# Layer 1's normalised inputs, from the third sequence on, transposed by VectorE in 32 x 32 squares that change places through DRAM instead of by TensorE

## The chip, the cores and the metric

The kernel runs on one core of a Trainium2 chip. The metric is the device time of one execution in microseconds (us). Engines are named as in the profile: PE is TensorE (PEld its weight loads), DVE is VectorE, ACT is ScalarE, POOL is GpSimd, SP is SyncE, which here only issues DMAs. SBUF is the memory on the core with 128 partitions, PSUM the accumulators of TensorE (8 banks of 128 x 512 f32), DRAM the memory off the core.

## What is computed

Two layers over x of shape (8, 512, 256): 8 sequences of 512 tokens with 256 channels, all f32. Layer 1 has causal attention with 16 heads of 64 and rotated queries and keys, and beside it a projection of the same normalised input in int8. Layer 2 has an attention of another kind and a gated network; the change does not touch what it computes. Cut to what matters:

```python
xn = layernorm(x)
q, k, v = xn @ Wq + bq, xn @ Wk + bk, xn @ Wv + bv          # 16 heads of 64
attended = softmax(causal(rope(q) @ rope(k).T / 8)) @ v
s = max(abs(xn).max() / 127, 1e-5)                          # over all sequences
quantised = (clip(round(xn / s), -128, 127) @ w8.T) * s * weight_scale + bias
x = x + attended @ Wo + bo + quantised                      # layer 1
yn = layernorm(x)
x = x + mask * softmax(left @ right.T / 16 + gate_bias) @ yn + gated(yn)   # layer 2
```

Every projection contracts over channels. A matmul of TensorE contracts over partitions, so the normalised input, which comes with tokens on partitions, is needed with channels on partitions: xnT, two halves k of 128 channels, each with 512 tokens along the partition. The projection of queries and keys streams xnT (the moving operand, with the weights stationary); the projection of values loads xnT as the stationary operand; the int8 projection uses a rounded and clipped copy of it as the stationary operand.

## The kernel before

The order of the instructions of each engine is the order of the program text; no scheduler moves anything within layer 1 and layer 2's body. An engine runs its instructions in that order and waits on semaphores; so does SP with its DMAs. All loads and stores below go through SP's one queue.

Layer 1 is a loop over 16 steps "at" (line 813), two for each sequence: b = at // 2 is the sequence, g = at % 2 the half of its heads. A step computes scores for its 8 heads in five runs, softens them (exponentials), turns the probabilities in squares of 32 on DVE (L551), and weighs the values of the step before. Between these lie the projections for later steps:

- project(at + 1, 0) makes queries for the next step, project_v(at + 1) its values, and project(at + 2, 1), near the end of the step, the keys of the step after next. All of these go through project_qk (L400 the matmuls, L405 their eviction by ACT, L407 four DMAs each that swap halves of heads) and project_v (L443 matmuls, L449 eviction, L450 a store to DRAM; load_v, L460, reads it back with 32 partitions to a DMA in the next step).
- prepare(b) normalises a sequence (L171) and takes the greatest magnitude (L301). From the fourth sequence on it runs in the step before its transposes; for the third it runs in the same step (at == 2), just ahead of them.
- transpose_x(b + 1) runs in the first step of a sequence (g == 0), after project_v(at + 1) and ahead of scores(at, 3): eight 128 x 128 transposes on PE (L318) into two PSUM banks, two copies by ACT into xnT (L321), and one DMA that keeps xnT in DRAM (keep_input, L310) for the int8 projection later. Then SP loads x of the next sequence (L80) into the only buffer that there is for x.

The first reader of the new xnT is project(at + 2, 1) of the same step, after scores(at, 3), scores(at, 4) and finish(at - 1) (L362, the output projection). xnT has two buffers (pool "big"), one for each of two sequences in flight.

The first two sequences are transposed ahead of the loop (lines 756 and 795). The kept inputs are read back much later: for sequences 0 and 1 in steps last - 3 and last - 2 (line 834), for sequence 2 in the last step (line 931), for the others in the loop of layer 2 (fetch_late). Each is rounded by POOL (L190), clipped by DVE (L196, L197) into bf16 and multiplied (L205). The buffer tag "xnl" holds such a late input; one of soften's tiles uses it once, in step 0.

Of the kernel before, what the change touches and what calls it, by code (L numbers as in the profile page):

```python
# [8 lines left out]
F32 = mybir.dt.float32  # L9
BF16 = mybir.dt.bfloat16  # L10
I8 = mybir.dt.int8
AF = mybir.ActivationFunctionType
ALU = mybir.AluOpType
# [3 lines left out]
P = 128  # L17
B, S, D = 8, 512, 256
H, L = 16, 64
NT = S // P  # L20
NK = D // P
# [8 lines left out]
Q = 32  # L30
# [10 lines left out]
ROUND = 12582912.0  # L41
# [3 lines left out]
def two_layers(  # L45
    ctx: ExitStack, tc, x, turns, Wq, Wk, Wv, Wo, w8, rows, sides, second, gates, out,
):
    nc = tc.nc
# [3 lines left out]
    big = ctx.enter_context(tc.tile_pool(name="big", bufs=2))  # L52
# [4 lines left out]
    far = ctx.enter_context(tc.tile_pool(name="far", bufs=1, space=bass.MemoryType.DRAM))  # L57
    ps = ctx.enter_context(tc.tile_pool(name="ps", bufs=8, space=PSUM))

    def bank(name):  # L60
        return ps.tile([P, S], F32, tag="b", name=name)

    def whole(name, columns=S):
        t = big.tile([P, NK * (S + 1)], F32, tag="big", name=name)
        return t[:, : NK * columns].rearrange("p (k n) -> p k n", k=NK)

    def tokens(b):
        return x[b].rearrange("(t p) c -> p t c", p=P)
# [2 lines left out]
        return xpool.tile([P, NT, D], F32, tag="x1", name=name, bufs=3)  # L71

    x1_far = [far.tile([P, NT * D], F32, name=f"x1f_{b}") for b in range(B - 1)]
    xn_far = [far.tile([P, NK * S], F32, name=f"xnf_{b}") for b in range(B)]

    def load_x(b, parts=1):
        t = xpool.tile([P, NT, D], F32, tag="x", name=f"x_{b}")
        for h in range(parts):
            rows = slice(h * NT // parts, (h + 1) * NT // parts)
            nc.sync.dma_start(t[:, rows, :], tokens(b)[:, rows, :])  # L80
        return t
# [8 lines left out]
    x_next = [load_x(0, 2)]  # L90
# [37 lines left out]
    w8b = const.tile([P, NK, D], BF16, name="w8b")  # L128
# [52 lines left out]
        nc.sync.dma_start(dst.rearrange("p t n -> p (t n)"), x1_far[b])  # L181

    def fetch_input(b, r):
        nc.sync.dma_start(r.rearrange("p a n -> p (a n)"), xn_far[b])
        return r

    def round_input(r):

        r = r.rearrange("p a n -> p (a n)")
        nc.gpsimd.tensor_scalar(r, r, xs[:, 1:2], ROUND, ALU.mult, ALU.add)  # L190

    def clip(r, xq):

        r = r.rearrange("p a n -> p (a n)")
        xq_ = xq.rearrange("p k n -> p (k n)")
        nc.vector.tensor_scalar(xq_, r, -ROUND, -128.0, ALU.add, ALU.max)  # L196
        nc.vector.tensor_scalar(xq_, xq_, 127.0, 127.0, ALU.min, ALU.min)  # L197

    def add_quantised(b, half, xq, u):
        rows = slice(2 * half, 2 * half + 2)  # L200
        acc = bank(f"acc_{b}_{half}").rearrange("p (j n) -> p j n", j=2)
        for j in range(2):
            tok = bass.ts(2 * half + j, P)
            for k in range(NK):
                nc.tensor.matmul(  # L205
                    acc[:, j, :], xq[:, k, tok], w8b[:, k, :], start=(k == 0), stop=(k == NK - 1)
                )
        u = u.rearrange("p (j n) -> p j n", j=2)
        for j in range(2):
            nc.vector.scalar_tensor_tensor(  # L210
                u[:, j, :], acc[:, j, :], xs[:, 0:1], rw[:, 0, :], ALU.mult, ALU.mult
            )
        nc.gpsimd.tensor_tensor(x1s[b][:, rows, :], x1s[b][:, rows, :], u, ALU.add)
# [41 lines left out]
    with ExitStack() as c0:  # L255
        c0.enter_context(tc.manual_schedule())

        def pool(name, bufs, **kw):
            return c0.enter_context(tc.tile_pool(name=name, bufs=bufs, **kw))

        work = pool("work", 1)
# [8 lines left out]
        wo = work.tile([P, NP, D], F32, name="wo")  # L270
# [15 lines left out]
        xnT = {}  # L286
        amax = work.tile([P, B], F32, name="amax")

        normed, seen = {}, {}
# [15 lines left out]
        def prepare(b):  # L305
            norm_input(b)
            greatest_of(b)

        def keep_input(b):
            nc.sync.dma_start(xn_far[b], xnT[b].rearrange("p k n -> p (k n)"))  # L310

        def transpose_x(b):
            xn = normed.pop(b)
            xnT[b] = whole(f"xnT_{b}")
            for k in range(NK):
                pb = bank(f"pxt_{b}_{k}")
                for t in range(NT):
                    nc.tensor.transpose(  # L318
                        pb[:, bass.ts(t, P)], xn[:, t, bass.ts(k, P)], ident
                    )  # L320
                nc.scalar.copy(xnT[b][:, k, :], pb)  # L321
            if b > 0:
                keep_input(b)

# [62 lines left out]
        def project_qk(at, which):  # L387


            b, g = divmod(at, NG)  # L390
            w = wqkv[which]

            l, y = (
                prob.tile([P, 2, S], F32, tag="p", name=f"{tag}_{at}_{which}") if at == 1 else
                work.tile([P, 2, S], F32, tag=tag, name=f"{tag}_{at}_{which}", bufs=2) for tag in "ly"
            )
            for t in range(2):
                pb = bank(f"pq_{at}_{which}_{t}")
                for k in range(NK):
                    nc.tensor.matmul(  # L400
                        pb, w[:, g, k, bass.ts(t, P)], xnT[b][:, k, :],
                        start=(k == 0), stop=(k == NK - 1),
                    )
                bias = BIAS + which * NP + 2 * g + t
                nc.scalar.activation(l[:, t, :], pb, AF.Identity, bias=cs[:, bias : bias + 1])  # L405
            for n in range(4):
                nc.sync.dma_start(y[bass.ts(n ^ 1, Q)], l[bass.ts(n, Q)])  # L407
            evicted[at, which] = l, y
# [25 lines left out]
        def project_v(at, halves=(0, 1)):  # L434
            b, g = divmod(at, NH)
            if 0 in halves:
                stores[at] = away.tile([4, P, NT * P], F32, tag="v", name=f"va_{at}")
            for half in halves:
                v = work.tile([P, 4, 2, P], F32, tag="v", name=f"v_{at}_{half}", bufs=2)
                for j in range(2):  # L440
                    pb = bank(f"pv_{at}_{half}_{j}")
                    for k in range(NK):
                        nc.tensor.matmul(  # L443
                            pb.rearrange("p (g n) -> p g n", g=2),
                            xnT[b][:, k, bass.ts(2 * half + j, P)],
                            wqkv[2][:, 2 * g : 2 * g + 2, k, :],
                            start=(k == 0), stop=(k == NK - 1),
                        )
                    nc.scalar.copy(v[:, :, j, :], pb.rearrange("p (r n) -> p r n", r=4))  # L449
                nc.sync.dma_start(  # L450
                    stores[at][:, :, half * 2 * P : half * 2 * P + 2 * P].rearrange("r p n -> p r n"),
                    v.rearrange("p r t n -> p r (t n)"),
                )
# [103 lines left out]
        half = S // Q // 2  # L557
# [28 lines left out]
        cuts = {}  # L586
# [7 lines left out]
        def by_tokens(t):  # L594
            return t.rearrange("p (t n) -> p t n", t=NT)

        late = {}

        def fetch_late(b):
            if b < B - 1:  # L600
                tag, k = {2: ("vr", 0), 3: ("vr", 1), 4: ("t1", 0), 5: ("t1", 1), 6: ("t2", 0)}[b]
                fetch_output(b, by_tokens(cuts[tag][k]))
            if b > 2:
                late[b] = fetch_input(b, cuts["wo"][b % 2].rearrange("p (k n) -> p k n", k=NK))

        def round_late(b):
            round_input(late[b])

        def clip_late(b):
            xq = work.tile([P, NK, S], BF16, tag="xq", name=f"xq_{b}")  # L610
            clip(late.pop(b), xq)
            return xq

# [199 lines left out]
        for at in range(1, last):  # L813
            b, g = divmod(at, NH)
# [16 lines left out]
            if at in (last - 3, last - 2):  # L831
                s_ = at - last + 3
                fetch_output(s_, output_tile(f"x1e_{s_}"))
                xnl = fetch_input(s_, work.tile([P, NK, S], F32, tag="xnl", name=f"xnl_{s_}"))
            divide(at, 0)
            turn_qk(2 * at + 3, 1)
            if at == last - 2:
# [19 lines left out]
            turn_qk(2 * at + 2, 0)  # L857
            turn(at, 1)
            if at in (last - 3, last - 2):
                xq = work.tile([P, NK, S], BF16, tag="xq", name=f"xq_{s_}")  # L860
                clip(xnl, xq)
            divide(at, 2)
            if at == 2:
                prepare(2)
            elif g == 1 and 1 <= b < B - 2:
                prepare(b + 2)
            if at == last - 1:
                turn_qk(2 * at + 3, 0)
            if at == 1:
# [2 lines left out]
            project_v(at + 1)  # L872
            if at == last - 1:
                break
            if g == 0 and b < B - 1:
                transpose_x(b + 1)
                if b + 2 < B:
                    x_next.append(load_x(b + 2))
            scores(at, 3)
            soften(at, 3)  # L880
            turn_qk(2 * at + 3, 0)
# [46 lines left out]
        divide(at, 1)  # L928
        keep_weighed(at - 1)
        load_v(at)  # L930
        late[2] = fetch_input(2, work.tile([P, NK, S], F32, tag="xnl", name="xnl_2"))
        add_biases(B - 1)
        turn(at, 0)
        scores(at, 2)
# [18 lines left out]
        r = gate(0)  # L953
        round_late(2)
        weigh(at)
        xq = clip_late(2)
# [10 lines left out]
        for b in range(B):  # L967
# [11 lines left out]
            if b > 0 and b + 2 < B:  # L979
                xq = clip_late(b + 2)  # L980
# [5 lines left out]
            else:  # L986
                r = gate(b)
# [90 lines left out]
```

## Time and profile before

| what | value |
|---|---|
| time, median of 3 runs | 941.17 us (938.4 to 942.62) |
| the profiled execution, own time | 939.1 us |
| its span, first to last instruction | 937.2 us |
| transposes L318 | 64, eight for each sequence, 0.27 us each (overlapping) |
| copies L321 | 16, 594 ns mean |
| matmuls L400 that stream xnT | 512 of 128 x 512, 227.5 us of PE's time together |
| matmuls L443 that load xnT as weights | 256, 114.3 us |
| DMA of xnT to DRAM (L310) | 8 of 512 KB, 3.3 us from issue to landing |

The profile is of one execution. A line of a timeline has the start in us, the time in us, the engine, the source line, the operation, what it writes and reads, the shape, and in brackets how long the engine sat idle before it and who ended that. A line of a group has the count, the busy time of the group in us and the mean of one in ns; groups of matmuls overlap in the pipeline, so the busy time is less than count times mean. A DMA's last number is the median time from issue to landing.

The steps with transposes of the third to eighth sequence begin at about 116, 209, 299, 388, 478 and 568 us of the span (their first scores); layer 2's loop runs from about 745 us to the end.

### The profile page before, as it was taken

To read this page: it belongs to the slowest core of one execution; us is meant where nothing else is said; L and a number is where in the kernel's file an instruction comes from. 1 tells how busy PE (TensorE), PEld (TensorE's weight loads), DVE (VectorE), ACT (ScalarE), POOL (GpSimd) and SP (SyncE) were. 2 spreads that over 40 slices of the span, in tenths; PEclk is the share of its full clock that TensorE was granted. 3 is DMA by queue.
4 is the path that set the end of the run, shared out by engine and by line. 5 is a ranking of instruction groups with operands and counts; after the bars stand their busy time and mean duration, and the time that the engine had idled before them with its cause. 6 is when DMAs were issued, how large, how long until landed. Compare 5 with 4: busy or idle time off the path is not lost.

```text
span 937.2 us, 27414 instructions
## 1 busy us (share of the span) xinstructions
PE 923.8 (99%) x10491; PEld 600.8 (64%) x10491; DVE 787.4 (84%) x2431; ACT 533.0 (57%) x1488; POOL 540.0 (58%) x688
## 2 busy tenths in 40 slices
PE   9998999999999999999999999999999999999998
PEld 5446565656666575757565656666657777777776
DVE  4998889898799889978997899899899588888854
ACT  3585555656575656474747566555667434445553
POOL 2676765655665757566665756678666424444311
PEclk9999999999999999999999999999999999999999
DMA  7667453525443545263535435453444132211011
GB/s 212 193 166 201 112 128 126 122 80 138 146 105 96 133 136 131 75 159 92 136 91 160 108 98 137 136 145 106 103 114 126 47 101 79 76 57 39 23 34 34
DMA packets 60930, 105.40 MB, mean 112 GB/s; under 512 B 7552, under 2 KB 38272, under 8 KB 60800
## 3 DMA queue, kind: packets, MB, share of 16 engines
q1 hardware_dynamic: 58928, 102.01, 40.1%
q10 hardware_dynamic: 1872, 1.64, 0.7%
q8 instruction: 83, 1.36, 0.6%
q14 instruction: 47, 0.39, 0.1%
HBM read 39.14 MB, written 28.84 MB: 73 GB/s over the span
## 4 chain that ended last, share of the span: by engine, by line
PE 92%; DVE 4%; issue 1%; ACT 1%; POOL 1%; SPq 0%; DMA 0%; DVEq 0%; ACTq 0%; POOLq 0%
PE pq L400 22%; PE av L568 14%; PE sc L480 13%; PE pw L362 12%; PE pv L443 10%; PE po L727 5%; PE pg L689 3%; PE pvv L701 3%; PE pk L674 3%; PE trc L714 1%; PE plr L240 1%; PE c L646 1%; DVE t L551 1%; PE acc L205 1%; DVE p L508 1%
## 5 line engine op out<-in xcount | busy, mean ns | idle before, releaser
L512 ACT ACTIVATE p<-p,nm 128x64 f32<-128x64 f32 (+15 forms) x512 | 259.9, 512 | 123.1 <-DVE nm L508 98.3
L531 POOL TENSOR_SCALAR p<-p,rs 128x512 f32<-128x512 f32 (+4 forms) x504 | 263.3, 543 | 44.0 <-DVE rs L523 41.9
L432 POOL TENSOR_TENSOR h<-h,y 128x1024 f32<-128x1024 f32 x62 | 161.0, 2596 | 188.9 <-DVE y L417 106.6
L508 DVE CUSTOM_DVE_ANT_0 p<-sc,cmask 128x64 f32<-128x64 f32 (+15 forms) x512 | 190.3, 434 | 61.5 <-PE sc L480 61.5
L551 DVE STREAM_TRANSPOSE t<-p 128x256 f32<-128x256 f32 (+3 forms) x640 | 192.1, 366 | 18.2 <-POOL p L531 18.1
L480 PE MATMUL sc<-h,h 64*32 64x416 f32 (+15 forms) x4096 | 138.7, 393 | 1.9 <-POOL h L432 1.2
L568 PE MATMUL av<-t,vr 32*64 32x192 f32 (+15 forms) x4096 | 128.8, 392 | 4.0 <-issue 4.0
L568 PEld LDWEIGHTS av<-t,vr 32*64 32x64 f32 x4096 | 123.2, 131 | 9.1 <-issue 7.8
L480 PEld LDWEIGHTS sc<-h,h 64*32 64x32 f32 x4096 | 78.8, 106 | 76.0 <-issue 56.5
L405 ACT ACTIVATE l<-pq,cs 128x512 f32<-128x512 f32 x128 | 84.7, 683 | 66.8 <-PE pq L400 54.4
L417 DVE TENSOR_TENSOR y<-y,cs 128x1024 f32<-128x1024 f32 x64 | 110.7, 1729 | 5.8 <-DMA y<-l 5.3
L362 PE MATMUL pw<-wo,att 128*128 128x256 f32 x512 | 114.8, 382 | 0.0
L400 PE MATMUL pq<-xnT,wq 128*128 128x512 f32 x256 | 114.6, 599 | 0.2 <-ACT xnT L321 0.2
L443 PE MATMUL pv<-wv,xnT 128*128 128x512 f32 x256 | 114.3, 599 | 0.0
L400 PE MATMUL pq<-xnT,wk 128*128 128x512 f32 x256 | 112.9, 593 | 0.6 <-DVE nm L508 0.6
L362 PEld LDWEIGHTS pw<-wo,att 128*128 128x128 f32 x512 | 95.9, 190 | 18.5 <-issue 6.1
L512 ACT ACTIVATION_READ_ACCUMULATOR p<-p,nm 128x1 f32 x512 | 97.3, 190 | 0.0
L400 PEld LDWEIGHTS pq<-xnT,wk 128*128 128x128 f32 x256 | 48.6, 190 | 56.6 <-issue 54.1
L443 PEld LDWEIGHTS pv<-wv,xnT 128*128 128x128 f32 x256 | 47.3, 190 | 57.9 <-issue 54.1
L417 DVE TENSOR_TENSOR h<-l,cs 128x1024 f32<-128x1024 f32 x64 | 79.5, 1243 | 4.5 <-ACT l L405 4.5
L400 PEld LDWEIGHTS pq<-xnT,wq 128*128 128x128 f32 x256 | 47.2, 190 | 56.0 <-issue 48.8
L582 ACT ACTIVATE att<-av,cs 128x512 f32<-128x512 f32 x64 | 38.7, 688 | 71.4 <-PE av L568 71.4
(113 smaller groups left out, 949.8 us busy)
## 6 DMA issues: line engine op xcount, KB each, us to landing
y<-l SPq DMA_DIRECT2D x256, 128.0 KB, 2.3
va<-v SPq DMA_DIRECT2D x32, 512.0 KB, 3.1
vr<-va SPq DMA_DIRECT2D x64, 256.0 KB, 4.8
x<-in_x SPq DMA_DIRECT2D x15, 512.0 KB, 4.2
xnf<-xnT SPq DMA_DIRECT2D x8, 512.0 KB, 3.3
x1f<-x SPq DMA_DIRECT2D x7, 512.0 KB, 2.7
out<-y SPq DMA_DIRECT2D x14, 256.0 KB, 2.2
cut_wo<-xnf SPq DMA_DIRECT2D x5, 512.0 KB, 4.2
```

The source lines that it names most:

```text
L362: nc.tensor.matmul(pw[:, j, :], atts[at, p][:, tok], wo[:, 4 * (at % NH) + p, :], start=(p == 0), stop=(p == 3),)
L400: nc.tensor.matmul(pb, w[:, g, k, bass.ts(t, P)], xnT[b][:, k, :], start=(k == 0), stop=(k == NK - 1),)
L405: nc.scalar.activation(l[:, t, :], pb, AF.Identity, bias=cs[:, bias : bias + 1])
L417: nc.vector.tensor_tensor(dst, src, table[:, None, :].to_broadcast([P, 2, S]), ALU.mult)
L432: (engine or nc.gpsimd).tensor_tensor(h, h, y, ALU.add)
L443: nc.tensor.matmul(pb.rearrange("p (g n) -> p g n", g=2), xnT[b][:, k, bass.ts(2 * half + j, P)], wqkv[2][:, 2 * g : 2 * g + 2, k, :], sta ...
L480: nc.tensor.matmul(scored[at, i][e][j * Q : j * Q + Q, :], q[rows, j % 2, bass.ts(i, Q)], k[rows, j % 2, :n], start=True, stop=True,)
L508: nc.vector.tensor_tensor_reduce(p[:, e, col : col + n], sc, cmask[:, S - n :], -1.0 / L**0.5, BIG, ALU.add, ALU.min, nm[:, c : c + 1],)
L512: nc.scalar.activation(p[:, e, col : col + n], p[:, e, col : col + n], AF.Exp, bias=nm[:, c : c + 1], scale=-1.0, accum_out=sm[:, c : c + 1],)
L531: nc.gpsimd.tensor_scalar(p, p, rs[:, c : c + 1], 1.0, ALU.mult, ALU.mult)
L551: nc.vector.transpose(turned[at][c][:, :, at_ : at_ + (n - 1) * pitch(c) + 1 : pitch(c), :], p[:, :, c * P : c * P + n * Q].rearrange("p e ...
L568: nc.tensor.matmul(banks[j][e * L : e * L + L, i * Q :], vs[at][rows, m, c, bass.ts(e, L)], t[c][rows, e, m * pitch(c) + m : m * pitch(c) ...
```

## The change

From the third sequence on, transpose_x is no longer called. In its place turn_x does three things. DVE transposes the normalised input in 32 x 32 squares with two instructions of 128 x 512 (one for each half of the channels), into a tile of tag "xnl" in which the element order along a partition is: block m of 32 channels, token r within the square, half k, tile t of 128 tokens. One DMA stores the tile to DRAM, and four DMAs, one for each group of 32 partitions, load it so that the squares change places: partition m * 32 + q receives, for each of the four blocks a of 32 partitions, 1 KB in a run. The store takes the place of keep_input, as the same bytes are read back for the int8 projection. On SP the four loads stand behind the landing of the store, and x of the sequence after stands behind the loads.

turn_x stands in the step ahead of project_v(at + 1), where transpose_x stood behind it. On PE nothing is in its place; on DVE it follows divide(at, 2) and prepare and goes before soften(at, 3); on SP it goes before the two stores of project_v.

The layout of xnT changes for all sequences: tokens lie n-major, (n k t) along the partition, so that two tokens that follow each other in a matmul's operand lie 8 elements (32 bytes) apart, where they were neighbours before. The first two sequences are still transposed by TensorE; ACT's copies now write in that layout, and keep_input takes four DMAs. fetch_input takes four DMAs for every late input. The int8 matmuls read their stationary operand with a step of 8 elements of bf16 (16 bytes).

```diff
-    xn_far = [far.tile([P, NK * S], F32, name=f"xnf_{b}") for b in range(B)]
+    xn_far = [far.tile([P, 4, NK * S // 4], F32, name=f"xnf_{b}") for b in range(B)]
...
     def fetch_input(b, r):
-        nc.sync.dma_start(r.rearrange("p a n -> p (a n)"), xn_far[b])
+        r_ = r.rearrange("p (a n) -> p a n", a=4)
+        for m in range(4):
+            nc.sync.dma_start(r_[bass.ts(m, Q)], xn_far[b][:, m].rearrange("(a k) n -> k a n", a=4))
         return r
...
+        xq_ = xq.rearrange("p (n k t) -> p n k t", n=P, k=NK)
         for j in range(2):
-            tok = bass.ts(2 * half + j, P)
             for k in range(NK):
                 nc.tensor.matmul(
-                    acc[:, j, :], xq[:, k, tok], w8b[:, k, :], start=(k == 0), stop=(k == NK - 1)
+                    acc[:, j, :], xq_[:, :, k, 2 * half + j], w8b[:, k, :],
+                    start=(k == 0), stop=(k == NK - 1),
                 )
...
+        def turned_input(b):
+            t = big.tile([P, NK * (S + 1)], F32, tag="big", name=f"xnT_{b}")[:, : NK * S]
+            xnT[b] = t.rearrange("p (n k t) -> p k t n", n=P, k=NK)
+            return t
+
+        def turn_x(b):
+            xn = normed.pop(b)
+            t = work.tile([P, 4, Q, NK, NT], F32, tag="xnl", name=f"xs_{b}")
+            for k in range(NK):
+                nc.vector.transpose(
+                    t[:, :, :, k, :].rearrange("p m r t -> p t m r"),
+                    xn[:, :, bass.ts(k, P)].rearrange("p t (m q) -> p t m q", m=4),
+                )
+            nc.sync.dma_start(
+                xn_far[b], t.rearrange("p m r k t -> p m (r k t)")
+            )
+            fetch_input(b, turned_input(b))
+
         def keep_input(b):
-            nc.sync.dma_start(xn_far[b], xnT[b].rearrange("p k n -> p (k n)"))
+            flat = kept.pop(b).rearrange("p (a n) -> p a n", a=4)
+            for m in range(4):
+                nc.sync.dma_start(
+                    xn_far[b][:, m].rearrange("(a k) n -> k a n", a=4), flat[bass.ts(m, Q)]
+                )
...
-            xnT[b] = whole(f"xnT_{b}")
+            kept[b] = turned_input(b)
...
-                nc.scalar.copy(xnT[b][:, k, :], pb)
+                nc.scalar.copy(xnT[b][:, k], pb.rearrange("p (t n) -> p t n", t=NT))
...
                     nc.tensor.matmul(
-                        pb, w[:, g, k, bass.ts(t, P)], xnT[b][:, k, :],
+                        pb.rearrange("p (t n) -> p t n", t=NT), w[:, g, k, bass.ts(t, P)], xnT[b][:, k],
                         start=(k == 0), stop=(k == NK - 1),
                     )
...
-                            xnT[b][:, k, bass.ts(2 * half + j, P)],
+                            xnT[b][:, k, 2 * half + j],
...
+            if g == 0 and b < B - 1:
+                turn_x(b + 1)
+                if b + 2 < B:
+                    x_next.append(load_x(b + 2))
             if at == last - 1:
                 turn_qk(2 * at + 3, 0)
...
             project_v(at + 1)
             if at == last - 1:
                 break
-            if g == 0 and b < B - 1:
-                transpose_x(b + 1)
-                if b + 2 < B:
-                    x_next.append(load_x(b + 2))
             scores(at, 3)
```

More of the change, by code (lines that the diff above doesn't have):

```diff
@@ L183, in fetch_input @@
     def fetch_input(b, r):
-        nc.sync.dma_start(r.rearrange("p a n -> p (a n)"), xn_far[b])
+        r_ = r.rearrange("p (a n) -> p a n", a=4)
+        for m in range(4):
+            nc.sync.dma_start(r_[bass.ts(m, Q)], xn_far[b][:, m].rearrange("(a k) n -> k a n", a=4))
         return r
     def round_input(r):
-        r = r.rearrange("p a n -> p (a n)")
         nc.gpsimd.tensor_scalar(r, r, xs[:, 1:2], ROUND, ALU.mult, ALU.add)
     def clip(r, xq):
[L194 to L197, printed above, removed]
+        nc.vector.tensor_scalar(xq, r, -ROUND, -128.0, ALU.add, ALU.max)
+        nc.vector.tensor_scalar(xq, xq, 127.0, 127.0, ALU.min, ALU.min)
     def add_quantised(b, half, xq, u):
@@ L307, in prepare @@
             greatest_of(b)
-        def keep_input(b):
-            nc.sync.dma_start(xn_far[b], xnT[b].rearrange("p k n -> p (k n)"))
+        def turned_input(b):
[14 more added lines that the diff above has]
+            fetch_input(b, turned_input(b))
+        def keep_input(b):
+            flat = kept.pop(b).rearrange("p (a n) -> p a n", a=4)
[3 more added lines that the diff above has]
+                )
+        kept = {}
         def transpose_x(b):
             xn = normed.pop(b)
-            xnT[b] = whole(f"xnT_{b}")
+            kept[b] = turned_input(b)
             for k in range(NK):
@@ L603, in fetch_late @@
             if b > 2:
-                late[b] = fetch_input(b, cuts["wo"][b % 2].rearrange("p (k n) -> p k n", k=NK))
+                late[b] = fetch_input(b, cuts["wo"][b % 2])
         def round_late(b):
@@ L609, in clip_late @@
         def clip_late(b):
-            xq = work.tile([P, NK, S], BF16, tag="xq", name=f"xq_{b}")
+            xq = work.tile([P, NK * S], BF16, tag="xq", name=f"xq_{b}")
             clip(late.pop(b), xq)
@@ L833, in two_layers @@
                 fetch_output(s_, output_tile(f"x1e_{s_}"))
-                xnl = fetch_input(s_, work.tile([P, NK, S], F32, tag="xnl", name=f"xnl_{s_}"))
+                xnl = fetch_input(s_, work.tile([P, NK * S], F32, tag="xnl", name=f"xnl_{s_}"))
             divide(at, 0)
@@ L859, in two_layers @@
             if at in (last - 3, last - 2):
-                xq = work.tile([P, NK, S], BF16, tag="xq", name=f"xq_{s_}")
+                xq = work.tile([P, NK * S], BF16, tag="xq", name=f"xq_{s_}")
                 clip(xnl, xq)
@@ L930, in two_layers @@
         load_v(at)
-        late[2] = fetch_input(2, work.tile([P, NK, S], F32, tag="xnl", name="xnl_2"))
+        late[2] = fetch_input(2, work.tile([P, NK * S], F32, tag="xnl", name="xnl_2"))
         add_biases(B - 1)
```

## The prediction

> **What bounds the kernel now.** I read the busy shares first, then the chain that ended last, then the engine timelines around one of the transposes that leave, then the rows that price what comes.
>
> ```profile
> span 937.2 us, 27414 instructions
> ...
> PE 923.8 (99%) x10491; PEld 600.8 (64%) x10491; DVE 787.4 (84%) x2431; ACT 533.0 (57%) x1488; POOL 540.0 (58%) x688
> ...
> PEclk9999999999999999999999999999999999999999
> ...
> PE 92%; DVE 4%; issue 1%; ACT 1%; POOL 1%; SPq 0%; DMA 0%; DVEq 0%; ACTq 0%; POOLq 0%
> ```
>
> TensorE is busy for 923.8 of 937.2 us at full clock, and 92% of the chain is its work: a microsecond taken from it is a microsecond off the end, unless something else then makes it wait. Between 237 and 610 us, where five of the six moved transposes lie, its busy time is 372.1 of 373.0 us. VectorE, at 84%, does not set the pace there, but it has to deliver in time.
>
> The timeline of TensorE around the fourth sequence's transposes, with VectorE's two lines from the same place:
>
> ```profile
> 230.48 7.13 PE L443 MATMUL pv<-wv,xnT 128*128 128x512 f32 x16
> 237.45 1.04 PE L318 MATMUL pxt<-ident,x 128*128 128x128 f32 x8
> 238.41 2.39 PE L480 MATMUL sc<-h,h 64*32 64x320 f32 x80
> 240.73 7.17 PE L362 MATMUL pw<-wo,att 128*128 128x256 f32 x32
> 247.75 7.03 PE L400 MATMUL pq<-xnT,wk 128*128 128x512 f32 x16
> ```
>
> ```profile
> 237.53 0.20 DVE L523 RECIPROCAL rs<-sm 128x4 f32<-128x4 f32 x2
> 239.60 0.49 DVE L508 CUSTOM_DVE_ANT_0 p<-sc,cmask 128x320 f32<-128x320 f32 x1 [1.88 <-PE sc L480]
> ```
>
> The eight transposes hold TensorE from 237.45 to 238.41: 0.96 us. The first reader of their result is the projection at 247.75. VectorE, after its reciprocals, waits 1.88 us for TensorE: the new work of VectorE falls into this hole.
>
> **What is removed.** For sequences three to eight, 48 transposes and 12 copies of ScalarE (594 ns mean each, 7 us in all). ScalarE is busy 57% and not on this part of the chain: its share counts as nothing. On TensorE the other gaps read as the first: 0.96 us at 326.80, 0.97 at 416.86, 506.93 and 596.70. Only the third sequence's place is longer, because its input is normalised late:
>
> ```profile
> 146.68 0.30 PE L318 MATMUL pxt<-ident,x 128*128 128x128 f32 x1 [0.51 <-PE pv L443]
> 147.23 0.33 PE L318 MATMUL pxt<-ident,x 128*128 128x128 f32 x1 [0.25 <-DVE x L171]
> 147.82 1.14 PE L318 MATMUL pxt<-ident,x 128*128 128x128 f32 x6 [0.26 <-DVE x L171]
> 148.89 2.39 PE L480 MATMUL sc<-h,h 64*32 64x320 f32 x80
> ```
>
> There the matmuls before end at about 146.1 (139.03 + 7.13), so 2.8 us go. The most that can be won is 5 x 0.96 + 2.8 = 7.6 us.
>
> **What is added, and whether it is in time.** Two transposes of 128x512 on VectorE, a store of 512 KB, which SP waits to land, four loads of 128 KB.
>
> ```profile
> L551 DVE STREAM_TRANSPOSE t<-p 128x256 f32<-128x256 f32 x448 | 161.1, 408 | 18.2 <-POOL p L531 18.1
> L551 DVE STREAM_TRANSPOSE t<-p 128x128 f32<-128x128 f32 x64 | 15.9, 268 | 0.0
> ```
>
> ```profile
> vr<-va SPq DMA_DIRECT2D x64, 256.0 KB, 4.8
> ...
> x1f<-x SPq DMA_DIRECT2D x7, 512.0 KB, 2.7
> ```
>
> 128 columns more cost 140 ns, so 512 columns cost 408 + 280 = 0.69 us, and two 1.38. They write with 32 bytes between neighbours, which no row here does; from above I take the dearest two-input row of 512 columns (L630, 1,019 ns): 2.04 for two. I take 1.38, since it is the same operation; both ends stay. The store looks like x1f<-x (4 KB a partition, nothing ahead of it in the queue): 2.7 us. The loads look like vr<-va, 32 partitions each: four of these at 264.76 land 4.2 to 5.7 us after their own issue, the last issue 1.33 us after the first, so 1 MB needs 7.0 us and the first 256 KB 4.2. Half the bytes should need some 4.2 to 4.5; from above, the 512 KB loads that met other traffic (x1e<-x1f, two of them) took 7.2.
>
> For the fourth sequence: VectorE is free at 237.65, done at 239.03, the store has landed at 241.8, the loads at 246.1 (0.1 us for each semaphore). TensorE, 0.96 earlier than before, asks for it at 247.75 - 0.96 = 246.8. It is hidden with 0.7 us to spare; with both dear ends it is 0.7 + 3.0 - 0.7 = 3.0 us late. The other four places have the same distance (9.4 us from scores to projection) and VectorE free at the same point, but the last, where the clip of VectorE ends at 598.1, has only 0.2 to spare. The third sequence misses: its normalising and the maximum (1.22 us) end at 149.4, transposes 150.8, store 153.6, loads 158.0, and TensorE would ask at 158.22 - 2.8 = 155.4. It waits 2.6 of the 2.8 us it won. If the wait is late, the projection, then the next scores and everything after them move by it.
>
> Sum of this part: -5 x 0.96 - 0.2 = -5.0 us.
>
> **What is queued behind.** SP now waits for VectorE and for the store, and behind it stand load_x of the next sequence and the two v stores. The v stores issue near 244 in place of 235.4 and 238.3, and are read by the load at 264.76; x is read one iteration later. Both have over 10 us to spare: nothing. If that cover went, a late v would hold the weighing (L568). VectorE's softening of the next scores starts 0.4 us later than the scores are ready; its next waits, on POOL for 1.06 us at 253.26 and on TensorE for 1.85 at 255.88, take that up: nothing. PSUM loses two allocations; iterations without transposes run that way already, with no idle time.
>
> **What is moved or reshaped.** The inputs now lie with 32 bytes between neighbouring tokens, for all eight sequences. ScalarE's four remaining copies write so: 0.59 us each, at most 0.74 (L621, the dearest copy-like row), two of them at the start, where TensorE waits: 0 to 0.3. Loads of the late inputs become four instead of one, SP issues at 0.33 to 0.5 us each; they have slack in layer 2 but little at the two places before its start: 0 to 2 us, I take 0.5. The 64 bf16 weight loads of L205 (98 ns) could grow to those of f32 (190): at most 64 x 0.06 = 4 us, as 130 ns of matmul cover them (8.3 us over 64); I take 0.
>
> The one large unknown is L400, where the input is streamed:
>
> ```profile
> L400 PE MATMUL pq<-xnT,wk 128*128 128x512 f32 x256 | 112.9, 593 | 0.6 <-DVE nm L508 0.6
> L443 PEld LDWEIGHTS pv<-wv,xnT 128*128 128x128 f32 x256 | 47.3, 190 | 57.9 <-issue 54.1
> ```
>
> Both halves of L400 hold TensorE 114.6 + 112.9 = 227.5 us, 0.44 each. No matmul here streams with a step. Below, it costs nothing: f32 streams at 0.44 us per 512 (0.87 ns a column) while bf16 of L205 moves a column in 0.51 ns, so a column of f32 leaves the memory more time than the array's fastest pace. Above, the slowest pace at which TensorE reads anything here is a weight load's, 190 ns for 128 columns, 1.48 ns a column: 512 x (0.76 - 0.44) = +163 us. I take nothing, since the pace of f32 is set by passes in the array more likely than by the reads; but 2.2% of L400 already eat the whole gain. L443 reads it as weights: 190 ns, hidden under 441 ns of matmul up to more than twice that.
>
> [...]
>
> **Sum.** -5.0 + 0.3 + 0.5 = -4.2 us on the profiled execution, whose time is 939.1 (span 937.2 and 1.9 around it): 934.9, or 0.45% less. It lies 2.1 below the median shown, so that median becomes 937.
>
> **Rivals.** (1) The round trip is late. For it: 512 KB loads of 7.2 us elsewhere, single DMA engines that land a microsecond after the others, strided writes on VectorE. Against: SP and the DMA queues are quiet here. Each microsecond of lateness in all six places gives 6 us; 1.5 late gives 941 + 9 - 5 = 945, all dear ends 941 + 18 - 5 = 954. (2) Slower: streaming with a step costs TensorE time at L400. It decides from 2.2%; each tenth is 23 us, the upper bound gives 937 + 163 = 1,100. For it: the layout changed for all sequences, and 24% of TensorE's time reads it. Against: the slack per f32 column. (3) The change does less than it says: the first two sequences stay on TensorE, and the third gives its gain back; this is in the sum.
>
> **Chances.** Forecast (hidden, free reads) 46%: own range 933 to 940. Late round trip 22%: 939 to 954. Slower reads 32%, of which 14% up to 990 and 18% beyond. A measurement here tells 0.5%, 4.7 us, from no change. Faster: 28 of the forecast's 46. Same: the other 18 and 9 of the second. Slower: 13 of the second and 32. The range goes from 932 (the full 7.6 us and a little scatter) to 990, leaving out 18% above and 2% below.
>
> **What would show it.** L318 drops to 16 instructions. L400's mean stays at 593 to 599 ns (if it rises, rival 2). At the projections of sequences four to eight TensorE has no wait on a DMA of xnT, at the third one of 2 to 3 us. The new transposes last 0.7 us. I am wrong if L400 grows, or if waits on xnT add up to over 7 us.

## The result and the profile after

The changed kernel takes 1,185.62 us (1,184.94 to 1,187.45, 4 runs) beside 940.5 us of the kernel before on the same chip: 1.261 of it, 95% interval 1.258 to 1.264. Slower by a quarter.

The page of the kernel after, its span, busy shares and chain:

```profile
span 1184.4 us, 27409 instructions
...
PE 1169.2 (99%) x10443; PEld 635.6 (54%) x10443; DVE 800.0 (68%) x2443; ACT 532.7 (45%) x1476; POOL 538.9 (45%) x688
...
PE pq L427 40%; PE av L595 11%; PE sc L507 10%; PE pw L389 7%; PE pv L470 6%; PE po L754 5%; PE pk L701 2%; PE pg L716 2%; PE pvv L728 2%; DVE t L578 2%; DVE p L535 2%; PE c L673 1%; PE trc L741 1%; PE plr L241 1%; DVE y L444 1%
```

TensorE is still busy 99% of the time, and one line has grown: the projection of queries and keys (L400 before, L427 now) had 22% of the chain and has 40%. Three groups of the kernel before, for comparison:

```profile
L400 PE MATMUL pq<-xnT,wq 128*128 128x512 f32 x256 | 114.6, 599 | 0.2 <-ACT xnT L321 0.2
L443 PE MATMUL pv<-wv,xnT 128*128 128x512 f32 x256 | 114.3, 599 | 0.0
L318 PE MATMUL pxt<-ident,x 128*128 128x128 f32 x64 | 9.1, 277 | 1.1 <-PE pv L443 0.5 <-DVE x L171 0.5
```

The groups that touch the new layout, after:

```profile
L427 PE MATMUL pq<-xnT,wq 128*128 128x512 f32 x256 | 239.4, 1102 | 0.7 <-ACT xnT L348 0.7
L427 PE MATMUL pq<-xnT,wk 128*128 128x512 f32 x256 | 238.4, 1098 | 6.0 <-DVE nm L535 4.2 <-DMA xnT<-xnf 1.4 <-DVE rs L550 0.4
L470 PE MATMUL pv<-wv,xnT 128*128 128x512 f32 x256 | 116.3, 607 | 0.0
L470 PEld LDWEIGHTS pv<-wv,xnT 128*128 128x128 f32 x256 | 79.0, 315 | 31.2 <-issue 5.2 <-ACT v L476 0.4
L321 DVE STREAM_TRANSPOSE xs<-x 128x512 f32<-128x512 f32 x12 | 12.8, 1148 | 0.0
```

The 512 matmuls that stream xnT hold TensorE 239.4 + 238.4 = 477.8 us where it was 227.5: +250.3. The group of L470 has 2.0 more. The 48 of 64 transposes that left had 9.1 x 48 / 64 = 6.8. That is +245.5, and TensorE's busy time grew by 1,169.2 - 923.8 = 245.4. Its idle time grew from 13.4 to 15.2. The span's 247.2 us are explained to a tenth.

TensorE's timeline of the kernel after in the step of the fourth sequence:

```profile
328.69 2.39 PE L507 MATMUL sc<-h,h 64*32 64x320 f32 x80
331.01 7.17 PE L389 MATMUL pw<-wo,att 128*128 128x256 f32 x32
339.40 14.91 PE L427 MATMUL pq<-xnT,wk 128*128 128x512 f32 x16 [1.21 <-DMA xnT<-xnf]
```

Sixteen matmuls of L427 took 7.03 us and take 14.91, and scores and output projection around them last as long as before. The wait of 1.21 us for xnT is the round trip. The landing of its store is recorded in 16 parts: fifteen were there at 333.46 us, the last at 335.13, and the loads were issued only then. The wait is small beside the 7.9.

### The profile page after: what moved, and what is told of

Read it like the earlier page. It is cut to its first block, busy times and chain, and to the rows that moved or that the text cites. A ratio compares the mean times of both kernels' runs of the same rounds, so it can differ in the third digit from the quotient of the medians.

```text
span 1184.4 us, 27409 instructions
## 1 busy us (share of the span) xinstructions
PE 1169.2 (99%) x10443; PEld 635.6 (54%) x10443; DVE 800.0 (68%) x2443; ACT 532.7 (45%) x1476; POOL 538.9 (45%) x688
## 4 chain that ended last, share of the span: by engine, by line
PE 91%; DVE 6%; DMA 1%; issue 1%; POOL 1%; SPq 0%; ACT 0%; DVEq 0%; POOLq 0%
PE pq L427 40%; PE av L595 11%; PE sc L507 10%; PE pw L389 7%; PE pv L470 6%; PE po L754 5%; PE pk L701 2%; PE pg L716 2%; PE pvv L728 2%; DVE t L578 2%; DVE p L535 2%; PE c L673 1%; PE trc L741 1%; PE plr L241 1%; DVE y L444 1%
## 5 line engine op out<-in xcount | busy, mean ns | idle before, releaser
L427 PE MATMUL pq<-xnT,wk 128*128 128x512 f32 x256 | 238.4, 1098 | 6.0 <-DVE nm L535 4.2
L427 PE MATMUL pq<-xnT,wq 128*128 128x512 f32 x256 | 239.4, 1102 | 0.7 <-ACT xnT L348 0.7
L432 ACT ACTIVATE l<-pq,cs 128x512 f32<-128x512 f32 x128 | 87.7, 686 | 308.8 <-PE pq L427 268.6
L427 PEld LDWEIGHTS pq<-xnT,wk 128*128 128x128 f32 x256 | 53.5, 211 | 168.2 <-issue 164.1
L507 PE MATMUL sc<-h,h 64*32 64x512 f32 (+15 forms) x4096 | 137.8, 393 | 1.1 <-POOL h L459 1.1
L427 PEld LDWEIGHTS pq<-xnT,wq 128*128 128x128 f32 x256 | 51.4, 206 | 160.6 <-issue 145.2
L595 PE MATMUL av<-t,vr 32*64 32x160 f32 (+15 forms) x4096 | 128.6, 392 | 1.0 <-issue 1.0
L470 PE MATMUL pv<-wv,xnT 128*128 128x512 f32 x256 | 116.3, 607 | 0.0
L470 PEld LDWEIGHTS pv<-wv,xnT 128*128 128x128 f32 x256 | 79.0, 315 | 31.2 <-issue 5.2
L444 DVE TENSOR_TENSOR h<-l,cs 128x1024 f32<-128x1024 f32 x64 | 81.8, 1278 | 19.1 <-ACT l L432 19.1
```

The costliest lines, as they stand in the source:

```text
L427: nc.tensor.matmul(pb.rearrange("p (t n) -> p t n", t=NT), w[:, g, k, bass.ts(t, P)], xnT[b][:, k], start=(k == 0), stop=(k == NK - 1),)
L444: nc.vector.tensor_tensor(dst, src, table[:, None, :].to_broadcast([P, 2, S]), ALU.mult)
L470: nc.tensor.matmul(pb.rearrange("p (g n) -> p g n", g=2), xnT[b][:, k, 2 * half + j], wqkv[2][:, 2 * g : 2 * g + 2, k, :], start=(k == 0), ...
L507: nc.tensor.matmul(scored[at, i][e][j * Q : j * Q + Q, :], q[rows, j % 2, bass.ts(i, Q)], k[rows, j % 2, :n], start=True, stop=True,)
L595: nc.tensor.matmul(banks[j][e * L : e * L + L, i * Q :], vs[at][rows, m, c, bass.ts(e, L)], t[c][rows, e, m * pitch(c) + m : m * pitch(c) ...
```

## The experiments

**The layout alone, at three distances.** Three kernels are the kernel before with all its transposes on TensorE, no turn_x, and only another order of the elements in xnT (and of the late inputs made from it). The edit of xnT against the kernel before (what stands behind # is a remark, not code of the kernel):

```diff
-            xnT[b] = whole(f"xnT_{b}")
+            flat[b] = big.tile([P, NK * (S + 1)], F32, tag="big", name=f"xnT_{b}")[:, : NK * S]
+            xnT[b] = flat[b].rearrange("p (n k t) -> p k t n", n=P, k=NK)    # 32 bytes from token to token
+            # "p (k n t) -> p k t n": 16 bytes;  "p (t n k) -> p k t n": 8 bytes
```

At 32 bytes: 

> The kernel before with the new layout of xnT alone: all 64 transposes stay on TensorE, no turn_x, no loads of xnT; only tokens lie 32 bytes apart, for the matmuls that stream xnT, the weight loads that read it and ScalarE's 16 copies that write it. Theory 1 (the step of the streamed operand is the whole loss): L400-type matmuls go from 0.44 to 0.93 us each, 512 of them, +250 us, so about 1,190 us. Theory 2 (the round trip over DRAM and its waits are the loss): no change, 941 us, L400 at 593 ns mean.

At 16 bytes: 

> As the layout-only kernel, but tokens 16 bytes apart. [...] Theory 1 as a matter of distance (cost grows with the step): clearly less than at 32 bytes, near 1,070. Theory 2: 941 us.

At 8 bytes: 

> As the layout-only kernel, but tokens 8 bytes apart, so that two columns share 16 bytes. [...] Theory 1 as any step at all: about 1,190 us. Theory 1 by distance: near 1,000. Theory 2: 941 us.

Measured: 1,186.97 us at 32 bytes (1.263, interval 1.261 to 1.266), 1,177.65 at 16 (1.253, 1.251 to 1.256), 948.74 at 8 (1.010, 1.009 to 1.012). The layout alone, without a single byte through DRAM on the way to the projection, costs what the whole change costs. The groups at 32 bytes, then at 16, then at 8:

```profile
L398 PE MATMUL pq<-xnT,wq 128*128 128x512 f32 x256 | 239.4, 1102 | 0.7 <-ACT xnT L319 0.7
L398 PE MATMUL pq<-xnT,wk 128*128 128x512 f32 x256 | 238.0, 1096 | 0.0
L441 PEld LDWEIGHTS pv<-wv,xnT 128*128 128x128 f32 x256 | 79.0, 315 | 31.3 <-issue 5.2 <-ACT v L447 0.4
L319 ACT COPY xnT<-pxt 128x512 f32<-128x512 f32 x16 | 16.9, 1173 | 7.4 <-PE pxt L316 7.4
```

```profile
L398 PE MATMUL pq<-xnT,wq 128*128 128x512 f32 x256 | 234.7, 1083 | 0.7 <-ACT xnT L319 0.7
L398 PE MATMUL pq<-xnT,wk 128*128 128x512 f32 x256 | 233.3, 1077 | 0.0
L441 PEld LDWEIGHTS pv<-wv,xnT 128*128 128x128 f32 x256 | 77.7, 310 | 32.4 <-issue 5.2 <-ACT v L447 0.4
L319 ACT COPY xnT<-pxt 128x512 f32<-128x512 f32 x16 | 17.1, 1195 | 7.5 <-PE pxt L316 7.5
```

```profile
L398 PE MATMUL pq<-xnT,wq 128*128 128x512 f32 x256 | 119.9, 618 | 0.3 <-ACT xnT L319 0.3
L398 PE MATMUL pq<-xnT,wk 128*128 128x512 f32 x256 | 118.2, 612 | 0.6 <-DVE nm L506 0.6
L441 PEld LDWEIGHTS pv<-wv,xnT 128*128 128x128 f32 x256 | 48.9, 196 | 56.6 <-issue 50.3 <-ACT p L510 5.8 <-ACT v L447 0.4
L319 ACT COPY xnT<-pxt 128x512 f32<-128x512 f32 x16 | 9.4, 651 | 7.9 <-PE pxt L316 7.9
```

The cost does not grow evenly with the distance. It jumps between 8 and 16 bytes: a matmul of L398 takes 465 ns at 8 bytes, 914 at 16 and 932 at 32, in place of 444 side by side (busy time over count). From 16 to 32 it grows by 2% of the group. Theory 2 falls, and so do growth with the distance (near 1,070 us at 16 bytes, near 1,000 at 8) and a loss at any step at all (about 1,190 at 8). A remainder stays at 8 bytes: 10.6 us of L398's time (119.9 + 118.2 - 227.5), which is that kernel's whole 1%. Where between 8 and 16 bytes the jump lies, and whether it depends on where the tile starts, is not shown: neither 12 bytes nor another start of the tile was tried.

**Runs of 32 tokens, the rest of the change kept.** The order along the partition becomes (k t r) within each 1 KB piece, so that the 32 tokens r of a square lie side by side. The DMAs stay as they are. The stationary operand is read with a single step, as in the changed kernel: project_v takes the 128 tokens of one block a as they lie (t r), and the values come out with blocks and tiles exchanged, which the load of v and one index in weigh undo; the clip writes its bf16 copy in plain order.

```diff
-            t = work.tile([P, 4, Q, NK, NT], F32, tag="xnl", name=f"xs_{b}")
+            t = work.tile([P, 4, NK, NT, Q], F32, tag="xnl", name=f"xs_{b}")
...
-            xnT[b] = t.rearrange("p (n k t) -> p k t n", n=P, k=NK)
+            xnT[b] = t.rearrange("p (a k t r) -> p k t a r", a=4, k=NK, t=NT)
+            runs[b] = t.rearrange("p (a k n) -> p a k n", a=4, k=NK)
...
-                            xnT[b][:, k, 2 * half + j],
+                            runs[b][:, 2 * half + j, k, :],
...
-                            vs[at][rows, m, c, bass.ts(e, L)],
+                            vs[at][rows, c, m, bass.ts(e, L)],
```

> The change with its transposes on VectorE and its way through DRAM, but with 32 tokens side by side in every place (a streamed operand in runs of 128 bytes, weight loads in runs of 512 bytes, VectorE's transposes writing runs of 32); the blocks of v come out in another order and are indexed so. Theory 1: L400-type matmuls return to 0.44 us, VectorE's transposes of 512 columns to 0.69 us; the time is that of before less 4 to 5 us for the transposes that TensorE no longer makes, plus what TensorE waits for xnT: 934 to 942 us. Theory 3 (not the step, but access patterns of more dimensions or data that came by DMA are slow): L400 stays near 1.1 us mean, about 1,185 us. Theory 2: 1,185 us.

Measured: 938.41 us, 0.9986 of before (0.9975 to 0.9998). Theory 3 falls: data that came by DMA, in a pattern of three dimensions, streams here at the pace of before when it lies in runs: 7.03 us for the 16 matmuls of L431 in the step of the fourth sequence (from 251.02 us on), as for those of L400. Two groups, and TensorE's timeline in the step of the third sequence with the window table's row for the projection there (its columns: us, busy time and instructions of PE, PEld, DVE, ACT and POOL, the granted clock of TensorE, DMA share, GB/s):

```profile
L431 PE MATMUL pq<-xnT,wk 128*128 128x512 f32 x256 | 116.0, 606 | 4.8 <-DVE nm L539 3.8 <-DMA xnT<-xnf 0.9
L325 DVE STREAM_TRANSPOSE xs<-x 128x512 f32<-128x512 f32 x12 | 7.7, 684 | 0.0
```

```profile
145.97 2.39 PE L511 MATMUL sc<-h,h 64*32 64x320 f32 x80
148.28 7.17 PE L393 MATMUL pw<-wo,att 128*128 128x256 f32 x32
158.80 10.03 PE L431 MATMUL pq<-xnT,wk 128*128 128x512 f32 x16 [3.34 <-DVE nm L539]
168.75 1.96 PE L511 MATMUL sc<-h,h 64*32 64x512 f32 x48
```

```profile
158.80:168.80 10.00, 10.00 (x23) 4.06 (x27) 5.04 (x17) 3.16 (x7) 6.97 (x14) 0.71 0.64 214
```

The third sequence's projection waits 3.34 us. The profile names DVE, but the last of the four loads of xnT was issued at 154.9 and took 3.7 us to land, at 158.6: it is the load. After the wait the same 16 matmuls take 10.03 us in place of 7.03, at a granted clock of 0.71. From the end of project_v (145.97, where the scores begin) to the end of this projection, this place takes 22.8 us. In the kernel before, with the transposes on TensorE, it took 19.1 us, from about 146.1 to 165.18:

```profile
158.22 7.03 PE L400 MATMUL pq<-xnT,wk 128*128 128x512 f32 x16
165.18 1.96 PE L480 MATMUL sc<-h,h 64*32 64x512 f32 x48
```

So the third sequence loses 3.7 us where 2.8 were to be won.

**The streamed operand alone, the weight loads alone.** In the kernel before, one operand reads with a step, and nothing else is touched:

```diff
-                        pb, w[:, g, k, bass.ts(t, P)], xnT[b][:, k, :],
+                        pb.rearrange("p (s n) -> p s n", s=8), w[:, g, k, bass.ts(t, P)],
+                        xnT[b][:, k, :].rearrange("p (n s) -> p s n", s=8),
```

> The kernel before, its layout and everything else kept, but the matmuls that stream xnT read their 512 tokens with a step of 8 (32 bytes); queries and keys come out with their tokens in another order, so the output is not the reference's. Weight loads and ScalarE's copies stay side by side. If the step of the streamed operand is the whole loss: 0.93 us for each matmul, about 1,188 us. If the weight loads and ScalarE's strided writes carried a share of the 247 us of the layout-only kernel: less by that share, 1,100 us or under.

```diff
-                            xnT[b][:, k, bass.ts(2 * half + j, P)],
+                            xnT[b][:, k, :].rearrange("p (n t) -> p t n", t=NT)[:, 2 * half + j],
```

> The kernel before, but the weight loads of project_v read their 128 tokens with a step of 4 (16 bytes); v comes out with its tokens in another order, so the output is not the reference's. Weight loads should take some 310 ns in place of 190. If they hide under the matmul before them (0.44 us): at most 2 us more, 940 to 943. If they do not: 256 x 0.12 = 31 us more, 971.

Measured: 1,185.78 us for the streamed operand (1.262, 1.258 to 1.266), 941.36 for the weight loads (1.001, 1.000 to 1.003). The groups of each, streamed operand first:

```profile
L400 PE MATMUL pq<-xnT,wq 128*128 128x512 f32 x256 | 239.5, 1103 | 0.2 <-ACT xnT L321 0.2
L400 PE MATMUL pq<-xnT,wk 128*128 128x512 f32 x256 | 238.1, 1098 | 0.0
```

```profile
L443 PEld LDWEIGHTS pv<-wv,xnT 128*128 128x128 f32 x256 | 77.7, 310 | 31.4 <-issue 4.1 <-ACT v L449 0.4
```

The step of the streamed operand is the whole loss. The weight loads, tried at 16 bytes, take 310 ns in place of 190 (315 at 32 bytes in the kernel after) and stay hidden but for 2.0 us: the group of L443 takes 116.3 us in place of 114.3. ScalarE's strided copies do not show either: the kernel of the streamed operand alone has none and is 1.2 us from the one that has them.

**What is left of the idea.** Two kernels build on the runs. In the first the third sequence goes back to TensorE; in the second turn_x of the fourth to seventh also stands earlier. The edit of the second, against the kernel after and beyond the runs:

```diff
             project(at + 1, 0)
+            if g == 0 and 1 < b < B - 2:
+                turn_x(b + 1)
+                x_next.append(load_x(b + 2))
...
-            if g == 0 and b < B - 1:
+            if at == last - 3:
                 turn_x(b + 1)
...
             if at == last - 1:
                 break
+            if at == 2:
+                transpose_x(2)
+                x_next.append(load_x(3))
```

> The kernel with runs of 32 tokens, but the third sequence, whose input is normalised just ahead, is transposed on TensorE again. If its late round trip (a wait of 3.3 us, and matmuls at a lower clock after it, 16 of L400's kind in 10.0 us in place of 7.1) is what ate the gain: 2.8 us of the transposes come back and some 6 go, 934.5 to 936.5 us, 0.995 to 0.997 of before. If the gain went elsewhere (VectorE's added work, DMA traffic): 938 to 940, no change to the kernel with runs.

> As the kernel before this one, and turn_x of sequences four to seven stands one projection earlier, behind project(at + 1, 0), so that xnT lands some 7 us ahead of its first reader. If single late DMA engines still cost waits at those places: another 1 to 2 us less, 933 to 935.5. If the round trip is hidden already: the same as the kernel before this one. If the store and loads now delay the v stores or the halves of q on SP: more, 936 to 942.

Measured: 938.06 us for the first (0.9983, 0.9972 to 0.9995) and 936.27 for the second (0.9957, 0.9943 to 0.9971). The first missed its range. Its profile shows what was expected at the third sequence (19.2 us for the place that took 22.8), and its span is 936.0 beside 938.2, yet the medians of the timed runs differ by 0.4 us only. Most of the 2.2 us between the spans is scatter: the profiled execution of the runs kernel took 939.98 us, 1.6 above its own median (12 runs from 936.3 to 941.34), the first's took 937.82, 0.2 below its median. Why a place that is 3.6 us shorter does not show in the medians stays open.

The second beats both kernels. It is 1.8 us below the first, as expected if late DMAs still cost waits (1 to 2 us less), but outside its range of 933 to 935.5, which was counted from the range that the first had missed. In the first's profile the fourth sequence's projection waits 1.0 us. The profile names another releaser, but xnT landed at 248.39, behind a store of 4.8 us:

```profile
248.53 7.10 PE L431 MATMUL pq<-xnT,wk 128*128 128x512 f32 x16 [1.00 <-DVE x L402]
```

The second's profile has no such wait. TensorE's timeline in its step of the fifth sequence has neither a wait nor transposes:

```profile
319.98 7.13 PE L474 MATMUL pv<-wv,xnT 128*128 128x512 f32 x16
327.04 2.39 PE L511 MATMUL sc<-h,h 64*32 64x320 f32 x80
329.36 7.17 PE L393 MATMUL pw<-wo,att 128*128 128x256 f32 x32
336.37 7.03 PE L431 MATMUL pq<-xnT,wk 128*128 128x512 f32 x16
```

Where weighing (L568, L599 with runs) begins, from the timelines, as a difference to the kernel before (us): in step 2, ahead of the third sequence's place, and in the step behind each of the six places, with the end of the span last:

```
step                        2      3      5      7      9     11     13   end
runs of 32               +1.0   +3.6   +3.3   +3.4   +1.9   +1.4   +1.2  +1.0
third on TensorE         +1.0   +0.3   +0.9   +1.2   -0.4   -0.8   -1.0  -1.2
and turn_x earlier       +0.8   -0.2   -0.8   -0.7   -1.9   -3.0   -3.2  -3.3
```

Each row is one execution, and some steps win nothing: waits of up to 1.1 us without a named releaser (before L599 or L568) fall in other places in each execution, and in the second row the wait of 1.0 us lies between steps 3 and 5. The last row wins 4.1 us from step 2 to the end, for five sequences of 0.96.

## Why the prediction was wrong, step by step

- **The step that failed** is the one on L400: "Below, it costs nothing", "I take nothing, since the pace of f32 is set by passes in the array more likely than by the reads". That weighing was my estimate; no run shows passes. The term was put at nothing and measured +250.3 us. What decided was there, as rival 2, at 32%: streaming with a step costs TensorE time, 914 and 932 ns a matmul at 16 and 32 bytes in place of 444, though at 8 bytes only 5% more (465 ns). A column of f32 streamed with 32 bytes between neighbours takes 0.93 us / 512 = 1.82 ns in place of 0.87. What I called slack (0.87 ns against 0.51 for bf16) was measured on columns side by side; it says nothing about columns that lie apart.
- **The upper bound failed too.** +163 us came from a weight load's 1.48 ns a column, taken for the slowest pace at which TensorE reads anything. But that load read neighbours. With a step, weight loads take 310 to 315 ns, 2.4 to 2.5 ns a column. A bound taken from rows that all lack the property in question bounds nothing. The range ended at 990 with 18% beyond; the time was 196 us beyond it.
- **VectorE's transposes**: 1.38 us for two with 2.04 as the upper bound. With the step the six pairs took 2.03 to 2.16 us (1,148 ns mean of one), at the bound or just past it; in runs one takes 684 ns. My 0.69 was right for the pattern that the row had; the step, which only the bound allowed for, was the case.
- **The third sequence**: wait of 2.6 us predicted, from loads landing at 158.0. In the kernel with runs they land at 158.6 and the wait is 3.34, in the kernel after 4.17. The mechanism was right and the size 0.7 us short in the runs kernel; what was missing is the low clock after it, 3.0 us over 16 matmuls there.
- **The other five**: hidden with 0.7 us to spare was nearly right in the runs kernel: one wait of 0.95 us in its profile, behind a store that took 4.4 us because the last of its 16 parts landed 1.8 us after the others. (VectorE was free at 237.72 by the lines shown, not at 237.65, so the margin was 0.6.) In the kernel after there were waits of 1.2, 0.2 and 0.4 us, each ending within 0.3 us of the landing of xnT. Rival 1 was real; at these five places it cost 1 to 2 us in each of the two kernels, and with the third sequence's wait 4 to 6, not 18.
- **Weight loads of L205**: 98 ns became 145 at 16 bytes; its matmuls take 8.4 us in place of 8.3. Nothing, as taken. **The late inputs**: none of TensorE's waits in the kernel after names them. SP's changed order cost nothing that shows.
- **What the sum would have been without the step**: the change in runs brings 1.2 us (938.41 beside 939.62), not 4.2. In its profile the third sequence loses 3.7 us where the sum had a gain of 0.2. Only with the third sequence left on TensorE and the rest started earlier does the idea bring 0.4% (0.9957), the size forecast for the change; that this is the same number is in part luck, since it is another kernel.

## What to carry to other kernels

Before an operand is laid out for a cheap DMA, ask how the engine that reads it most will walk it, and count those reads: 512 matmuls paid 0.49 us each for a layout that was to save 0.96 us in five places and 2.8 in a sixth. At the matmul here, 8 bytes between f32 neighbours cost 5% (465 ns in place of 444), 16 bytes more than as much again (914), runs of 32 elements nothing (114.6 us for the 256 matmuls that make queries, as before): where there is a choice, take the runs. Where the other reader then cannot take the elements in order, permute its output's tokens and undo it where data is reloaded anyway, as the runs kernel does with v. And where no row of a profile has the new property, a bound from rows without it is no bound; leave the range open on that side.

## What the hardware showed

Time of one instruction by the distance of neighbouring elements in SBUF. A matmul's is its group's busy time over its count, the others are means:

```
                                   side by side   8 bytes   16 bytes   32 bytes   extra a column at 32
matmul streams 512 columns, f32       444 ns       465        914        932        0.95 ns
weight load of 128 columns, f32       190          196        310        315        0.98
ScalarE writes 512 columns, f32       594          651       1195       1173        1.13
VectorE transposes 512 columns, f32   684 (runs)     -          -       1148        0.91
weight load of 128 columns, bf16       98          114        145          -           -
```

The numbers are of the kernel before and the three kernels of the layout alone; VectorE's are of the kernel with runs of 32 and the kernel after, and 145 of the kernel after. The bf16 weight loads also take 98 ns at 4 bytes. In these runs three engines, reading or writing, took nearly the same 0.9 to 1.1 ns more for each f32 element at 32 bytes than for one side by side.

In this one case the strided stream did not follow TensorE's clock. In the kernel after, the third sequence's projection stands behind a wait of 4.17 us and runs at a mean granted clock of 0.82 (0.50 until 222 us, 1.00 from 223), and its 16 matmuls take 15.02 us, nearly as long as at full clock (14.91). In the runs kernel a clock of 0.71 stretched the same 16 from 7.03 to 10.03. That the memory and not the array sets the strided pace is an estimate from these two places; it was not tried by itself.

```profile
217.15 15.02 PE L427 MATMUL pq<-xnT,wk 128*128 128x512 f32 x16 [4.17 <-DVE nm L535]
```

```profile
217.00:232.00 15.00, 14.85 (x16) 3.93 (x16) 4.82 (x17) 2.94 (x7) 6.76 (x13) 0.82 0.46 147
```
